# Relational graph convolution on one core: 43 of the 196 octets of layer 2 take their rows from h in the chip's memory instead of by gathers

## The chip, the cores and the metric

One NeuronCore of a Trainium2 chip runs the whole program. The metric is the device time of one execution in microseconds (us); the kernel before takes 4593.86 us (median of 3 runs, 4577.43 to 4597.59).

## The reference

There are 12,500 nodes with 128 features and 200,000 edges, sorted by destination, each with one of 8 relations. Each of two layers computes, for every node and relation, the mean of the messages that arrive there, and sums the eight means; the weights of a relation are a mix of 8 basis matrices.

```python
def _rgcn_conv(x, src, dst, et, basis, comp, root, bias):
    W = jnp.einsum('rb,bio->rio', comp, basis)
    xw = jnp.einsum('ni,rio->nro', x, W)
    msgs = xw[src, et]
    seg = dst * N_REL + et
    summed = jax.ops.segment_sum(msgs, seg, num_segments=N_NODES * N_REL)
    cnt = jax.ops.segment_sum(jnp.ones((msgs.shape[0],), x.dtype), seg, num_segments=N_NODES * N_REL)
    mean = summed / jnp.maximum(cnt, 1.0)[:, None]
    agg = mean.reshape(N_NODES, N_REL, HIDDEN).sum(axis=1)
    return agg + x @ root + bias
...
for l in range(N_LAYERS):
    h_new = _rgcn_conv(h, src, dst, edge_type, basis[l], comp[l], root[l], bias[l])
    h_new = jax.nn.relu(h_new)
    h = h_new + h
...
x = _layernorm(x + h, axis=-1)
```

## The kernel before

**Tiling.** The edges lie in 1563 columns of 128, and eight columns (1024 edges) are an octet; there are 196 octets, the last one of three columns. 98 blocks of 128 nodes cover the nodes. The edges are in the order of their destinations, so an octet reaches some 64 neighbouring nodes, and two octets about one block.

**Layer 1** (loop over o). `gather` (L651) has POOL issue eight indirect DMAs for an octet (L677), each of 128 rows of x. `onehot` (L1098) has DVE write for each column a 128x128 one-hot over (relation, one of 16 node slots), times the edge's weight 1/count (L1121), and one 128x256 one-hot `pl` (L1129) that says where the octet's node slots lie in a window of 256 nodes. `means` (L1206) multiplies rows by one-hots (PE, L1214), ACT copies the sums (`take_means`), `product` (L1238) multiplies by the eight relation matrices (L1246), `place` (L1258) adds the result into the window (L1277), and `finish` (L1285) adds bias, ReLU and residual. The new h lies in the `arena` tile as hT, features on partitions and nodes along the free axis. `table(j)` (L1335) multiplies block j of hT by all eight matrices of layer 2 in two halves of four relations (L1345, 512 columns each, through the PSUM banks pt and ct) and stores them in DRAM as `y_d`, one row for each node and relation. Halves wait in the list `tables`; from octet 50 on one is taken in each octet, and a second one while more than six wait or after octet 180. What is left over is done after the loop by `table_now`.

**Layer 2** (loop over q). An octet's eight gathers now take rows of `y_d` by 8*source + relation, so there is no product left. `slot_hots` (L1085) writes eight 128x32 one-hots (L1090) and one `pl` (L1093); `slot_sums` (L1433) adds rows into slots with eight matmuls of 32 stationary columns (L1441), four output quarters of 32 partitions, in a quarter of the bank po1 (`misc`); ACT copies them to `ys`; one octet later `place_sums` (L1451) adds them into the window (L1466), with a root matmul (L1470) in every other octet. `open_block` (L1415) copies a block of hT for that and for the residual; `norm` (L1558) turns eight finished blocks back (L1573) and normalizes them. From octet 192 on `add_rows` (L1476) does the sums.

**What sets the order.** `Plan.add` (L327) emits every instruction in program order on its engine and makes the semaphore waits from the named cells that it reads and writes. Gathers are issued five octets ahead (`gathers`, L697) into a ring of seven `rows` tiles, through four semaphore lanes `gq`, one octet each: an octet's first gather waits until the octet four before it has landed. The gathers of the last six octets of a layer also wait for PE's sums up to that point (`done`) and are issued two octets ahead. Layer 2's octets from the third on wait for all of `y_d`.

Of the kernel before, what the change touches and what calls it, by code (L numbers as in the profile page):

```python
# [300 lines left out]
class Plan:  # L301
# [90 lines left out]
    last = None  # L392
# [37 lines left out]
def ordered_path(  # L430
# [63 lines left out]
    assert FULL == NQ - 4  # L494
    main = slice(HALO, HALO + P)
# [57 lines left out]
    def h_cells(j):  # L553

        return [("h", j)] + [c for a, b, cells in over.values() if a < (j + 1) * P and b > j * P for c in cells]

    comp_sb = keep([P, L * R * NB], F32, "comp_sb")
    first = keep([P, B], F32, "first")
# [36 lines left out]

    fails = keep([P, B + 4], F32, "fails")
    fix = keep([P, 3], F32, "fix")
# [53 lines left out]
    def gather(l, q):  # L651
        if q >= NQ:
            return
# [410 lines left out]
    def check_all():  # L1064
        pt, pc = pt_b
        pb = pt.rearrange("p b t -> p (b t)")
        pe(lambda: nc.tensor.matmul(pb[0:1, :B + 4], ones, fails, start=True, stop=True),
           ["ones"] + [("fails", b) for b in range(B + 4)], [pc])
        vec(lambda: nc.vector.tensor_reduce(nb_f, pb[0:1, :B + 4], axis=AX.X, op=ALU.max), [pc], ["nb_f"])
        vec(lambda: nc.vector.tensor_copy(bad, nb_f), ["nb_f"], ["bad"])  # L1070
# [27 lines left out]
    def onehot(l, q, g=None):  # L1098

        if l == 1 and q < FULL:  # L1100
# [7 lines left out]
        if q >= NQ and (g is None or g < 0):  # L1108
            return
        emits, reads, cells = [], ["cols"], []  # L1110
# [224 lines left out]
    def table(j):  # L1335
# [29 lines left out]
        if not split:  # L1365
# [7 lines left out]
             (s_b[1][0].rearrange("p t d -> p (t d)")[:, :2 * P], s_b[1][1])]  # L1373

    sT_all = [t.rearrange("p r g k -> p (r g k)") for t in sT_r.tiles]
    yr_all = [t.rearrange("p r d -> p (r d)") for t in yr_r.tiles]
    homes = {"idx": idx.bitcast(F32), "kr": kr, "sT0": sT_all[0], "sT1": sT_all[1], "yr0": yr_all[0], "yr1": yr_all[1],
             "iota": iota_f, "dm": dm_t.rearrange("p b c -> p (b c)")}
# [7 lines left out]
    def home(where, n, *cell):  # L1386
# [4 lines left out]
        return homes[where][:, a:a + n], cell  # L1391

    dm2_t = [home("sT0", Q * 2 * K, "dm2", i) for i in range(3)]
    pl2_t = [(t, ("pl2", i)) for i, t in enumerate(pl_r.tiles)] + [home("iota", 2 * P, "pl2", 3)]
# [4 lines left out]
    dm_home_c = [c for c in old if old[c] == homes_c["dm"]]  # L1399
    dms2 = {}  # L1400
    hb_b = [(t, ("hb", i)) for i, t in enumerate((id_k, id_r, jmp.bitcast(F32)))]
    old.update({("hb", i): ["id_k", "id_r", "jmp"] for i in range(3)})
    touched = set()
# [7 lines left out]

    hb = {}
    misc = po_b[1]

    def open_block(k):  # L1415
        n = rows_of(k)
        t, c = hb_b[k % 3]
        copy(t[:, :n], hT[:, k * P:k * P + n], [("h", k)], new(c))
        plan.mark("ACT")
        hb[k] = t, c  # L1420

    def slot_numbers():
# [8 lines left out]
        plan.mark("DVE")  # L1431

    def slot_sums(q):  # L1433
        t, c = rows_g.pop((1, q))
        d, dc = dms2.pop(q)
        b, bc = misc
        m0 = b[:, 3, :]
# [13 lines left out]
    def place_sums(q, k, opens, last):  # L1451
# [4 lines left out]
        reads = [c, oc]  # L1456
        m = P
        if root_in:
# [157 lines left out]
    def sup(q):  # L1616
        return (q * Q + G) // (2 * G) - 1
# [57 lines left out]
    def checks():  # L1675
        weights(1, (pt_b, pt_b))
        yield
        for b in range(B):
            yield from check_edges(b)
        yield from check_span()  # L1680
        yield from check_place()
        yield from fix_list()

    later = checks()
# [32 lines left out]
    for o in range(NG - 3):  # L1717
# [11 lines left out]
        if parts is None:  # L1729
            run(later, 1)  # L1730
        if not opened:
# [21 lines left out]
        for i in range(2):  # L1753
            if turned_to:
                here = pt_b
                a, b = turned_to.pop(0)
            elif tables and o >= TABLE and (i == 0 or len(tables) > 6 or o > NG - 16):
                here = (pt_b, ct_b)[i]
                a, b = tables.pop(0)(here)
            else:  # L1760
                break
# [3 lines left out]
            if b is not None:  # L1765
                copies.append(b)
        plan.mark("PE")
    plan.lazy = False
# [65 lines left out]
    for q in range(2):  # L1834
        onehot(1, q)
    open_block(0)
    plan.lazy = True
# [3 lines left out]
    for q in range(NQ):  # L1841
# [38 lines left out]
        if todo:  # L1880
            todo.pop(0)()
# [90 lines left out]
```

## Time and profile before

| | |
|---|---|
| median of 3 runs | 4593.86 us |
| the profiled execution | 4590.46 us, its span 4588.4 us |
| busy in the span | PE 1941.5, DVE 1384.9, ACT 466.3, POOL 2953.3 us |
| mean granted TensorE clock | 0.665 |

The span runs from the first to the last instruction; some 2 us of the execution lie around it. PE is TensorE's matmuls, PEld its weight loads, which overlap them; DVE is VectorE, ACT is ScalarE, POOL is GpSimd, and SP issues plain DMAs. A float32 matmul shows as two records, and so does its weight load. In a row of a grouped view stand the line, engine, operation, output and inputs, shape and count, then busy time and mean length, then the idle time just before the group and what ended it. A releaser "remote", or "an unknown queue" in the chain, is here a DMA of the gathers' queue. The clock is the share of full speed that the throttle granted to TensorE.

### The profile page before, as it was taken

Reading aid. Unit: us, or ns where it says so; the run is one execution under the profiler, and the core shown is the slowest. Engines: PE = TensorE matmul, PEld = TensorE weight load, DVE = VectorE, ACT = ScalarE, POOL = GpSimd, SP = SyncE. Lnnn points to the kernel's source line nnn. Section 1 sums busy time; section 2 is a strip of 40 time slices with the busy share of each in tenths; the row PEclk is TensorE's granted clock in tenths of the full one; section 3 lists DMA queues with packets and bytes.
Section 4 is the critical chain, followed back from the end, with each engine's and each line's share of the span. In section 5 each row is a group of like instructions: output and inputs, shape, how many; then the busy total and the mean of one; then the engine's idle time right before and its main releaser. Section 6 shows DMA issues by size and latency. Waiting matters only on the chain.

```text
span 4588.4 us, 33820 instructions
## 1 busy us (share of the span) xinstructions
PE 1941.5 (42%) x11751; PEld 1512.2 (33%) x11751; DVE 1384.9 (30%) x4891; ACT 466.3 (10%) x1141; POOL 2953.3 (64%) x3135
## 2 busy tenths in 40 slices
PE   2666756666566666656731122222222222222213
PEld 1555555555455555545521111111111111111112
DVE  2544333333333323233321222222222222222224
ACT  0111112121111111111210000000000000000000
POOL 5666666666666666666556666666666666666665
PEclk9878778787777777777865555555555555555556
DMA  3111122232222222222221111212212212122121
GB/s 100 45 50 46 46 62 87 87 92 92 88 69 73 74 69 74 64 66 70 78 71 45 47 51 52 56 46 57 55 47 55 56 47 56 46 56 55 47 55 50
DMA packets 129812, 284.69 MB, mean 62 GB/s; under 512 B 54019, under 2 KB 61773, under 8 KB 129637
## 3 DMA queue, kind: packets, MB, share of 16 engines
q0 software_dynamic: 100064, 205.13, 17.2%
q10 hardware_dynamic: 16971, 52.05, 3.0%
q1 hardware_dynamic: 12602, 25.31, 1.6%
q8 instruction: 94, 1.54, 0.1%
q14 instruction: 81, 0.66, 0.0%
HBM read 223.63 MB, written 58.65 MB: 62 GB/s over the span
## 4 chain that ended last, share of the span: by engine, by line
another core or an unknown queue 64%; PE 20%; issue 8%; ACT 5%; DVE 2%; DMA 0%; POOL 0%; SPq 0%; ACTq 0%; POOLq 0%; DVEq 0%
PE y L1246 7%; PE s L1214 5%; ACT sT L627 2%; PE pt L1345 2%; PE po L1441 2%; ACT ys L627 1%; PE po L1277 1%; DVE dm L1121 1%; ACT y_row L627 1%; PE ct L1345 1%; PE ct L870 0%; PE po L1279 0%; PE ct L871 0%; PE pt L1183 0%
## 5 line engine op out<-in xcount | busy, mean ns | idle before, releaser
L677 POOL DMA_INDIRECT rows<-in_x_dram,idx x1563 | 1476.1, 944 | 841.7 <-issue 440.2
L677 POOL DMA_INDIRECT rows<-y_d,idy x1563 | 1475.1, 944 | 742.6 <-issue 453.3
L1441 PE MATMUL po<-rows,sT 128*32 128x128 f32 x3072 | 206.3, 411 | 1571.3 <-ACT ys L627 1151.2
L1246 PE MATMUL y<-w_sb,sT 128*128 128x128 f32 x3136 | 542.3, 345 | 526.2 <-ACT ys L627 198.6
L1246 PEld LDWEIGHTS y<-w_sb,sT 128*128 128x128 f32 x3136 | 509.4, 254 | 551.6 <-ACT ys L627 207.6
L1121 DVE TENSOR_SCALAR dm<-cols,kr,w 128x128 f32<-128x128 f16 x1563 | 526.2, 403 | 494.2 <-remote 203.1
L1441 PEld LDWEIGHTS po<-rows,sT 128*32 128x32 f32 x3072 | 121.9, 155 | 1658.1 <-ACT ys L627 1190.5
L1090 DVE TENSOR_SCALAR sT<-cols,kr,w 128x32 f32<-128x32 f16 x1536 | 352.8, 303 | 762.9 <-remote 617.7
L1214 PEld LDWEIGHTS s<-dm,rows 128*128 128x128 f32 x3126 | 436.3, 217 | 161.0 <-ACT sT L627 86.5
L1214 PE MATMUL s<-dm,rows 128*128 128x128 f32 x3126 | 450.5, 302 | 64.9 <-ACT sT L627 40.8
L627 ACT ACTIVATE sT<-s 128x512 f32<-128x512 f32 x391 | 212.5, 596 | 783.0 <-remote 556.8
L627 ACT ACTIVATE ys<-po 128x128 f32<-128x128 f32 x192 | 53.2, 277 | 2087.1 <-remote 1936.5
L1298 DVE TENSOR_TENSOR s<-s,carry 128x128 f32<-128x128 f32 x97 | 28.9, 298 | 670.8 <-remote 455.7
L1298 DVE TENSOR_TENSOR po<-po,carry 128x128 f32<-128x128 f32 x98 | 29.2, 298 | 655.1 <-remote 454.7
L1345 PE MATMUL pt<-w_sb,arena 128*128 128x512 f32 x258 | 157.3, 682 | 62.4 <-issue 50.0
L1466 PE MATMUL s<-pl,ys 128*128 128x256 f32 x288 | 167.9, 684 | 0.0
L1277 PE MATMUL po<-pl,ys 128*128 128x256 f32 x392 | 139.4, 440 | 24.2 <-issue 15.8
L627 ACT ACTIVATE y_row<-pt 128x512 f32<-128x512 f32 x131 | 78.4, 598 | 682.0 <-remote 484.2
L870 PE MATMUL ct<-arena,id_h 128*128 128x512 f16 (+1 forms) x188 | 75.5, 421 | 84.4 <-DVE arena L860 37.1
L860 DVE TENSOR_TENSOR arena<-cols,arena 128x129 f16<-128x129 f16 (+62 forms) x188 | 73.6, 408 | 69.5 <-remote 65.5
L1129 DVE TENSOR_SCALAR pl<-cols,pos 128x256 f32<-128x256 f16 x196 | 93.1, 476 | 0.0
L1466 PEld LDWEIGHTS s<-pl,ys 128*128 128x128 f32 x288 | 69.7, 301 | 53.3 <-issue 53.3
(212 smaller groups left out, 1409.7 us busy)
## 6 DMA issues: line engine op xcount, KB each, us to landing
y_d<-y_row ACTq DMA_DIRECT2D x96, 512.0 KB
rows<-in_x_dram,idx POOLq DMA_INDIRECT x1563
rows<-y_d,idy POOLq DMA_INDIRECT x1563
x_g<-in_x_dram SPq DMA_DIRECT2D x24, 512.0 KB
out_dram<-x_g SPq DMA_DIRECT2D x12, 512.0 KB
arena<-in_L_gnn_basis_dram SPq DMA_DIRECT2D x2, 512.0 KB
w_d<-y_row SPq DMA_DIRECT2D x2, 512.0 KB
w_sb<-w_d SPq DMA_DIRECT2D x2, 512.0 KB
```

The costliest lines, as they stand in the source:

```text
L627: act(lambda: nc.scalar.activation(out_t, in_t, AF.Copy), reads, writes)
L677: ins.append(nc.gpsimd.indirect_dma_start(out=t[:, i - q * Q, :], out_offset=None, in_=table_t, in_offset=bass.IndirectOffsetOnAxis(ap=ids ...
L870: nc.tensor.matmul(ct[:, :nb, :], id_h, eq[:, s - s0, :nb, main], start=(s == 1), stop=False)
L1090: vec(in_turn([lambda i=i: nc.vector.tensor_scalar(t[:, i, :], cols[:, :2 * K], kr[:, i0 + i:i0 + i + 1], w[:, i0 + i:i0 + i + 1], op0=ALU ...
L1121: emits.append(lambda i=i: nc.vector.tensor_scalar(t[:, i - q * Q, :wide], cols[:, :wide], ids[:, i:i + 1], w[:, i:i + 1], op0=ALU.is_equa ...
L1129: emits.append(lambda: nc.vector.tensor_scalar(o[:m], cols[:m], pos[:m, g // (2 * R), g % (2 * R):g % (2 * R) + 1], None, op0=ALU.is_equal))
L1214: last = nc.tensor.matmul(s_b[i // 4][0][:, i % 4, :], t[:, i, :], d[:, i, :], start=True, stop=True)
L1246: last = nc.tensor.matmul(y[:m], t[:, r, :nt, :].rearrange("p t k -> p (t k)"), w_sb[:, 0, r, :], start=(r == 0), stop=(r == R - 1))
L1277: ins = nc.tensor.matmul(a, o[:m], t[:m], start=opens, stop=last and not root_in)
L1345: pe(lambda: nc.tensor.matmul(hb[:n].rearrange("p r d -> p (r d)"), hT[:, j * P:j * P + n], w_sb[:, 1, k * H:(k + 1) * H, :].rearrange("p ...
L1441: last = nc.tensor.matmul(m0[i // 2 * 2 * K:(i // 2 + 1) * 2 * K, :], d[:, i, :], t[:, i, :], start=i % 2 == 0, stop=i % 2 == 1)
L1466: ins = nc.tensor.matmul(a, o[:m], t[:m], start=opens, stop=last and not root_in and not fixed)
```

## The change

In layer 2 the octets 20, 24, ..., 188 (`ROUTED`, 43 of them) issue no gathers. Their sums are formed from h itself, before the relation matrices, in these steps.

- **Sort, in layer 1** (octets 88 to 174, one half octet of four columns in each). `groups_of` compares the number of each edge's source block with 0 to 99, `earlier_of` counts with triangular and all-ones matmuls in float16 how many earlier edges of the octet have the same block, `ranks_of` takes the edge's rank and makes one-hots of 32 columns times three values (node in the block, segment, count), and `slots_of` adds these into 100 blocks x 32 slots, which two DMAs store to DRAM. Before that `values` prepares the three values. In octets 86 to 175 the second table half is not taken. `check_ranks` covers the capacity of 32 slots.
- **Turn h back** (`turn_blocks`, octets 0 to 12 of layer 2): 98 transposes put h in place as rows of nodes; `open_block` turns a block once more for its own use.
- **A unit for each routed octet**, seven steps spread over four octets from octet 13 on. A step has four tiles of four blocks (the seventh has one tile of two blocks). `compare` makes one-hots of 32 columns for 16 blocks at once (128x512) from a broadcast of the slots' node numbers (`fetch`, 128 times 6400 bytes); `pick_rows` has 16 matmuls with 32 stationary columns that pick each slot's row of h; `slots_in` makes for each tile a 128x640 one-hot over two batches of 512 edges, 8 relations and 40 node slots, times the weight; `add_up` multiplies each tile by the two halves of it (320 columns) into two PSUM banks; after the 25th tile ACT copies both, and `relate` multiplies by the eight relation matrices. `place_sums` then takes 80 instead of 128 slots.
- `slot_sums` writes to the bank ct instead of po1.

```diff
+    BT = 4
+    CAP = 32
+    NW = 40
+    BU = P // CAP
+    NTL = -(-NT // BU)
+    TU = 4
+    NU = -(-NTL // TU)
+    NGR = NTL * BU
+    SEG = R * NW
+    BR = 2
+    EVERY = 4
+    TURN = 8
+    FROM = -(-NT // TURN)
+    ROUTED = list(range(FROM + 10 * EVERY // NU + 2, 192, EVERY))
+    NR = len(ROUTED)
+    SORT = 88
...
     def gather(l, q):
-        if q >= NQ:
+        if q >= NQ or l == 1 and q in ROUTED:
             return
...
+    def groups_of(x):
...
+        vec(lambda: nc.vector.tensor_tensor(
+            o3, cols[:, None, :NGR].to_broadcast([P, BT, NGR]), g.unsqueeze(2).to_broadcast([P, BT, NGR]),
+            op=ALU.is_equal), ["cols", grp_b[1]], [oc])
...
+    def earlier_of(x):
...
+        def emit():
+            last = nc.tensor.matmul(c3, tri, o3, start=True, stop=False)
+            for k in range(BT if h else 0):
+                nc.tensor.matmul(c3, every, f3[:, k:k + 1, :].to_broadcast([P, BT, NGR]), start=False, stop=False)
+            for k in range(1, BT):
+                last = nc.tensor.matmul(c3[:, k:, :], every, o3[:, :BT - k, :], start=False, stop=k == BT - 1)
+            return last
...
+    def ranks_of(x):
...
+        vec(lambda: nc.vector.tensor_tensor(c3, b3, o3, op=ALU.mult), [bc, oc], [cc])
+        vec(lambda: nc.vector.tensor_reduce(rk, c3, axis=AX.X, op=ALU.add), [cc], [rc])
+        vec(lambda: nc.vector.tensor_tensor(
+            j3, cols[:, None, :CAP].to_broadcast([P, BT, CAP]), rk.unsqueeze(2).to_broadcast([P, BT, CAP]),
+            op=ALU.is_equal), ["cols", rc], [jc])
+        vec(lambda: nc.vector.tensor_tensor(
+            v4, j3[:, :, None, :].to_broadcast([P, BT, 3, CAP]),
+            val[:, j, ts].unsqueeze(3).to_broadcast([P, BT, 3, CAP]), op=ALU.mult), [jc, val_b[1]], [vc])
...
+    def compare(t):
+        i, u = t // NU, t % NU
...
+        vec(lambda: nc.vector.tensor_scalar(o[:, :n], b.bitcast(F16)[:, u * HC:u * HC + n], node_p, None,
+                                            op0=ALU.is_equal), [bc, "node"], new(oc))
+
+    def slots_in(t):
...
+        for v, m in tiles_at(u):
+            o, oc = slot_b[(i * NTL + v) % len(slot_b)]
+            n = m * CAP
+            vec(lambda v=v, o=o, n=n: nc.vector.tensor_scalar(
+                o[:n], segs[:n], sg[:n, v:v + 1], sg[:n, NTL + v:NTL + v + 1], op0=ALU.is_equal, op1=ALU.mult),
+                [segs_b[1], sgc], new(oc))
+
+    def pick_rows(t):
...
+        b, bc = pt_b
+        def emit():
+            for x, (v, m) in enumerate(at_u):
+                for k in range(m):
+                    j = v * BU + k
+                    n = rows_of(j)
+                    c = (x * BU + k) * CAP
+                    last = nc.tensor.matmul(b[k * CAP:(k + 1) * CAP, x, :], o[:n, c:c + CAP],
+                                            hT[:n, j * P:(j + 1) * P], start=True, stop=True)
+            return last
...
+        copy(g[:m, :n * P], b[:m, :n, :].rearrange("p t d -> p (t d)"), [bc], new(gc))
+
+    seg_b = [y_full, po_b[0]]
+
+    def add_up(t):
...
+            for x, (v, m) in enumerate(at_u):
+                o, n = slot_b[(i * NTL + v) % len(slot_b)][0], m * CAP
+                for k, (b, _) in enumerate(seg_b):
+                    last = nc.tensor.matmul(b.rearrange("p t d -> p (t d)")[:, :SEG], g[:n, x * P:(x + 1) * P],
+                                            o[:n, k * SEG:(k + 1) * SEG], start=v == 0, stop=v == NTL - 1)
...
+    def route_step(t):
+        i, u = t // NU, t % NU
+        if u == 0 and i < NR:
+            unit_rows(i)
+        compare(t + 1)
+        if i < NR:
+            pick_rows(t)
+        if 0 <= t - 1 < NR * NU:
+            slots_in(t - 1)
+        if 0 <= t - 2 < NR * NU:
+            add_up(t - 2)
+        if u == 3 and i >= 1 and i - 1 < NR:
+            relate(i - 1)
+        if u == 1:
+            fetch_rows(i + 1)
+        if u == NU - 1:
+            fetch(i + 2)
+
+    steps_of = {}
+    for t in range(NR * NU + 5):
+        steps_of.setdefault(FROM + t * EVERY // NU, []).append(t)
...
     def slot_sums(q):
...
-        b, bc = misc
+        b, bc = ct_b
...
             elif tables and o >= TABLE and (i == 0 or len(tables) > 6 or o > NG - 16):
+                if i == 1 and SORT - 2 <= o < SORT + 2 * NR + 2:
+                    break
...
+        if 0 <= o - SORT < 2 * NR:
+            earlier_of(o - SORT)
+        if 0 <= o - SORT - 1 < 2 * NR and (o - SORT) % 2 == 0:
+            slots_of((o - SORT) // 2 - 1)
...
+        turn_blocks(q)
+        if q == FROM - 1:
+            compare(0)
+        route(q, 0)
         late = q - 1
-        if q < FULL:
+        if q < FULL and q not in ROUTED:
             slot_sums(q)
         if 0 <= late < FULL:
             place_sums(late, sup(late), *opened_by(late))
         if q >= FULL:
             add_rows(q, k, opens, last)
+        route(q, 1)
         onehot(1, q + 2)
         if sup(q + 2) != sup(q + 1) and q + 2 < NQ:
             open_block(sup(q + 2))
+        route(q, 2)
```

More of the change, by code (lines that the diff above doesn't have):

```diff
@@ L1108, in onehot @@
         if q >= NQ and (g is None or g < 0):
+            return
+        if l == 1 and q in ROUTED:
+            i = ROUTED.index(q)
+            o, c = pl[q] = pl2_r.take()
+            vec(lambda: nc.vector.tensor_scalar(o[:2 * NW], cols[:2 * NW], pos2[:2 * NW, i:i + 1], None,
+                                                op0=ALU.is_equal), ["cols", "pos2"], new(c))
+            plan.mark("DVE")
             return
@@ L1391, in home, with spare @@
         return homes[where][:, a:a + n], cell
+    def spare(n, *cell):
+        old[cell] = room_c + [rank_b[1] + (x,) for x in range(2 * NR)]
+        return later_on(n), cell
+    bits_b = [spare(NGR * CAP // 2, "bits", i) for i in range(2)]
+    hot_b = [home("dm", HC, "hot", i) for i in range(3)]
+    rows_b = [home("dm", HC, "picked", i) for i in range(3)]
+    slot_b = [spare(2 * SEG, "slot", i) for i in range(5)]
+    slot_b += [home(("sT1", "idx", "idx")[i], 2 * SEG, "slot", 5 + i) for i in range(3)]
+    sum_b = [home(("yr0", "yr1")[i], R * BR * NW, "sum", i) for i in range(2)]
+    segs_b = home("yr1", SEG, "segs")
+    rows2_b = [home("dm", P, "rows2", i) for i in range(2)]
     dm2_t = [home("sT0", Q * 2 * K, "dm2", i) for i in range(3)]
@@ new lines, in ordered_path, with relate @@
+    for i in range(2):
+        for k in range(BR):
+            old[sum_b[i][1] + (k,)] = old[sum_b[i][1]]
+    def relate(i):
+        t_s, sc = sum_b[i % 2]
+        t4 = t_s.rearrange("p (r b n) -> p r b n", r=R, b=BR)
+        b, bc = misc
+        pe(in_turn([lambda r=r: nc.tensor.matmul(
+            b[:BR * NW, 0, :], t4[:, r].rearrange("p b n -> p (b n)"), w_sb[:, 1, r, :], start=r == 0, stop=r == R - 1)
+            for r in range(R)]), [sc + (k,) for k in range(BR)] + [("w", 1, r) for r in range(R)], [bc])
+        plan.mark("PE")
+        o, c = ys[ROUTED[i]] = ys_r.take()
+        copy(o[:BR * NW], b[:BR * NW, 0, :], [bc], [c])
+        plan.mark("ACT")
```

273 lines of the change are left out of this document (263 added, 10 removed).

## The prediction

> **What bounds the kernel now.** I read the page first, then layer 2 by stretches.
>
> ```profile
> span 4588.4 us, 33820 instructions
> ...
> PEclk9878778787777777777865555555555555555556
> ...
> L677 POOL DMA_INDIRECT rows<-y_d,idy x1563 | 1475.1, 944 | 742.6 <-issue 453.3
> ```
>
> The profiled execution took 4590.46 us, 2.1 us more than this span and 3.4 us less than the median of the runs shown. My sum is made against it. From about the middle the granted clock is 0.5, and POOL has one kind of work, the gathers. The next rows are two stretches of the view by stretches (busy us of PE, PEld, DVE, ACT, POOL, then clock, DMA share, GB/s): the steady part of layer 2, and ten microseconds at the end of layer 1.
>
> ```profile
> 2600.00:4400.00 1800.00, 399.47 (x3104) 246.06 (x3103) 466.55 (x1936) 62.93 (x249) 1196.61 (x1269) 0.52 0.19 52
> 2240.00:2250.00 10.00, 10.00 (x71) 8.37 (x70) 6.12 (x20) 4.68 (x10) 0.00 (x0) 1.00 0.18 72
> ```
>
> In layer 2 PE is busy 22% of the time at a clock of 0.52, DVE 26%, ACT 3%. In 1800 us there are 1269 gathers, one in 1.418 us, so an octet of eight takes 11.35 us. The groups of that stretch say why:
>
> ```profile
> L677 POOL DMA_INDIRECT rows<-y_d,idy x1269 | 1197.6, 944 | 603.7 <-issue 367.3 <-remote 234.9 <-PE po L1441 0.6
> ```
>
> A gather costs 0.944 us plus 0.29 us of issue (367.3/1269), some 9.9 us an octet. The other 1.5 us an octet (234.9 over 158.6 octets) is the wait for the octet four before to land. Everything else waits for these gathers. The stretch that the change replaces runs from octet 13's sums to octet 187's:
>
> ```profile
> L1441 PE MATMUL po<-rows,sT 128*32 128x128 f32 x2784 | 187.7, 413 | 1385.5 <-ACT ys L627 1051.4 <-issue 299.5 <-DVE x_g L1581 34.6
> ```
>
> ```profile
> 2559.20 0.46 PE L1441 MATMUL po<-rows,sT 128*32 128x128 f32 x4
> ```
>
> ```profile
> 4512.84 0.67 PE L1441 MATMUL po<-rows,sT 128*32 128x128 f32 x16
> 4513.43 0.70 PE L1466 MATMUL s<-pl,ys 128*128 128x256 f32 x2
> 4513.97 0.38 PE L1470 MATMUL s<-jmp,w_sb 128*128 128x128 f32 x2
> 4514.28 0.66 PE L1441 MATMUL po<-rows,sT 128*32 128x128 f32 x16
> ```
>
> The first row is the group of `slot_sums` in that stretch, the others are its ends in the order of time (start and length in us). At 16 records an octet these are 174 octets, in 4514.3 - 2559.2 = 1955.1 us: 11.24 us each.
>
> **The change: what goes.** 43 of these octets lose eight gathers. Were gathers all, 131 octets at 11.35 us would take 1487 us and 468 us would go. Four octets would need 34.0 instead of 45 us. But PE has to do a whole unit in the same four octets, so PE's work must be priced, and at the clock that it then has.
>
> **The price of a matmul.** At 2240 us PE is dense, and its clock is 1.00. The order of time there:
>
> ```profile
> 2240.14 1.02 PE L1345 MATMUL ct<-w_sb,arena 128*128 128x512 f32 x2
> 2241.00 1.95 PE L1214 MATMUL s<-dm,rows 128*128 128x128 f32 x16
> 2242.78 1.95 PE L1246 MATMUL y<-w_sb,sT 128*128 128x128 f32 x16
> 2244.57 0.60 PE L1277 MATMUL po<-pl,ys 128*128 128x256 f32 x2
> 2245.00 1.02 PE L1345 MATMUL pt<-w_sb,arena 128*128 128x512 f32 x2
> ```
>
> Start to start (a length also holds the drain), a float32 matmul (two records) over 512 columns takes 0.86 us, over 256 0.43, over 128 0.223 (1.78 for eight). It goes with the columns, so 320 columns take 0.5375 us. Weight loads hide. For 32 stationary columns I take octet 186, in the four rows from 4512.84 us above; the view by stretches has it at full clock too:
>
> ```profile
> 4512.84:4514.88 2.04, 2.04 (x38) 1.47 (x37) 2.04 (x10) 0.28 (x1) 0.00 (x0) 1.00 0.00 0
> ```
>
> Sixteen such records take 0.59 us, where one after the other they would need 16 x 0.111 = 1.78 us. So the four output quarters run side by side, 0.028 us a record. The matmuls after them take 0.54 and 0.31 us instead of 0.43 and 0.22; this switch between narrow and full belongs to the block, which costs 0.79 us.
>
> **PE's sum.** Per unit: `pick_rows` has six blocks of 32 records, 0.79 + 16 x 0.028 = 1.24 us each, and a small one of 0.6, together 8.0 us. `add_up` has 25 tiles x 2 = 50 matmuls over 320 columns, 26.9 us. `relate` has eight of 128, 1.8, and `unit_rows` about 0.2. That makes 36.9 us, and 43 units 1587 us. Beside them, in the same 174 octets: 131 `slot_sums` at 0.79, 103 us; 174 `place_sums` at 0.43, 75; a root matmul and the new turn of `open_block` in every other octet, 87 x 0.44, 38; the transposes of `norm`, eight in 16 octets, 19. All of it is **1822 us** at full clock, 41.9 us in four octets, against 1955 now. Against 34 us of gathers PE sets the pace, and gathers run ahead of it.
>
> **What PE waits for on top.** Matmuls of a step follow an order laid out by hand. `pick_rows(t)` needs the one-hot that DVE made a step before, `add_up(t-2)` a copy by ACT two steps old and one-hots that DVE could begin two steps before, as eight slot tiles hold two steps. A step is six microseconds of PE, so these have time; what is queued behind PE's waits, the next gather octet's sums, has landed by then. The places where PE must wait are the shared banks: `misc` after an `open_block` or a `norm` turn (the reader's 0.3 to 0.7 us, a few times a unit) and pt after the short seventh step, whose picks wait for ACT's copies of two banks and one of 0.6 us. No row has such waits; bounds are nothing and one step's one-hots from DVE, 2.2 us, plus those, some 3.5 us. I take **1.5 us a unit**, 65 us, since each wait is short and the queue orders agree.
>
> **DVE and ACT beside it.**
>
> ```profile
> L1121 DVE TENSOR_SCALAR dm<-cols,kr,w 128x128 f32<-128x128 f16 x1563 | 526.2, 403 | 494.2 <-remote 203.1 <-PE pt L1345 94.8 <-PE ct L1345 79.4
> L1090 DVE TENSOR_SCALAR sT<-cols,kr,w 128x32 f32<-128x32 f16 x1536 | 352.8, 303 | 762.9 <-remote 617.7 <-PE po L1441 64.5 <-PE s L1466 53.6
> ...
> L1581 DVE TENSOR_TENSOR x_g<-po,x_g 128x512 f32<-128x512 f32 x24 | 16.6, 692 | 159.6 <-PE po L1573 98.5 <-remote 53.6 <-issue 7.5
> ...
> L832 DVE CAST arena<-arena 128x512 f32<-128x512 int32 x3 | 1.2, 415 | 0.0
> ...
> L1427 DVE TENSOR_SCALAR idx<-idx 128x1664 int32<-128x1664 int32 x1 | 1.0, 1028 | 0.0
> ```
>
> ```profile
> L1601 DVE TENSOR_SCALAR x_g<-x_g,st 128x128 f32<-128x128 f32 x8 | 2.1, 363 | 0.0
> ```
>
> Between SBUF tiles a column costs 0.53 ns ((1028-415)/1152), and eight two-scalar operations of 128 columns take 2.1 us. So 640 columns in `slots_in` take 0.27 + 512 x 0.53 = 0.54 us. No row has float16 in and float32 out between SBUF tiles; from PSUM (L1090, L1121) a column costs 1.04 ns, which makes 0.87 us the upper bound. I take 0.54, as the operands lie in SBUF. A unit then costs DVE 25 x 0.54 = 13.6, seven comparisons at 0.42 = 2.9, and the octets' own work, 2.94 us each in the stretch of 1800 us, less a routed octet's eight one-hots (8 x 0.23): 9.9 us. Together 26 us of 42, or 36 by the upper bound. ACT gets seven copies of 0.6 us and some short ones, 7 us of 42. Both are hidden while their order holds.
>
> **Layer 1.**
>
> ```profile
> 1000.00:1800.00 800.00, 494.78 (x2637) 412.05 (x2636) 254.02 (x808) 139.88 (x301) 526.22 (x558) 0.77 0.26 77
> ...
> 2320.00:2340.00 20.00, 1.67 (x7) 0.76 (x5) 0.00 (x0) 0.28 (x1) 14.88 (x17) 0.61 0.20 53
> ```
>
> 558 gathers in 800 us make 11.5 us an octet; PE is busy 7.1 and DVE 3.6 us of it. The sort adds five DVE operations of 128 to 400 columns, some 2.6 us by L1581's 692 ns, and on PE a mean of 1800 float16 columns and half of eight short matmuls, some 1.5 us. DVE reaches 6.2 and PE 8.6 of 11.5, so the gathers hide both. The list of table halves, counted octet by octet from the two rules, stands at 26 instead of 7 in octet 172, and at 12 instead of none after the loop. Ten halves more at 0.86 us of PE and 0.6 us of ACT are some 15 us; PE is idle for 18 of 20 us at 2320, where it waits for the last gathers, so most of it is hidden. I add **8 us** for that and the small preparations (bounds 0 and 20). The broadcast of 0.8 MB a unit is small beside a DMA share of 0.19.
>
> **The sum.** 4588.4 - 1955.1 + 1822 + 64.5 + 8 = 4527.8, and 2.1 around the span: **4530 us**, 1.3% below 4590.5.
>
> **Two rules of the skill.** The Trainium skill's page "TensorE: Matmul & The Clock Gate" (What's actually happening) says that TensorE starts throttled to half speed and is released by some 3.4 us of activity; the rows at 0.52 and 1.00 agree, and by that rule a dense unit keeps 1.00. "SBUF — State Buffer" (Who interferes with whom), also in the Trainium skill, speaks against the change: a VectorE operation between SBUF tiles in a two-port mode locks GpSimd out entirely while it runs.
>
> **Rivals.**
>
> *The clock falls back* (12%). PE's waits in each step are spread, and the dense stretch shown at 1.00 is ten microseconds long. In layer 1, with PE busy 62%, the clock is 0.77. The streaming part goes with 1/clock: at 0.9 it takes 2025 us, and the time is 4733; at 0.77, 2367, and 5075. It decides below 0.97. Against it: PE's work is 96% of the new stretch.
>
> *PE and DVE in lockstep* (18%). DVE works strictly in order, and operations of `finish` and `norm` that wait for PE stand ahead of `slots_in`. If in each unit PE waits out one whole step's one-hots and the banks, 3.7 us, the time is 4530 + 43 x 2.2 = 4625, slower; with the upper bound for DVE (four at 0.87, so 5 us) 4681. It decides from 2.9 us a unit, 0.4 us a step. For it: one order, three engines. Against it: DVE has 16 us to spare.
>
> *The gathers are held up by DVE* (5%). If POOL stands still in every operation between SBUF tiles, a unit's 24 gathers at 1.24 us and 16.5 us of such operations make 46.3 us, 11.6 for each octet of the stretch: 174 octets take 2014 us, the time is 4657. That is the page's rule on the two ports at its full. The trace shows little of it:
>
> ```profile
> 2930.20 2.14 DVE L1601 TENSOR_SCALAR x_g<-x_g,st 128x128 f32<-128x128 f32 x8
> 2930.88 0.99 POOL L677 DMA_INDIRECT rows<-y_d,idy  x1 [0.30 <-issue]
> 2932.18 0.98 POOL L677 DMA_INDIRECT rows<-y_d,idy  x1 [0.31 <-issue]
> ```
>
> Under eight such operations in a row, two gathers took 0.99 and 0.98 instead of 0.94 us.
>
> *It doesn't do what it says* (2%). If a check of the sort (32 slots a block, 40 nodes a batch) fails, the program runs the general path behind it; at four indirect DMAs a column, 6252 at 1.24 us, that adds over 7700 us. Some 10 edges a block make this unlikely.
>
> **How the numbers follow.** The forecast, PE dense at full clock with 0 to 3.5 us of waits a unit, has 62% (4457 to 4616), and 1% is left for what I don't see. A measurement of this kernel can tell about 0.5% from no change, 23 us: the forecast's part below 4567 needs waits under 2.4 us a unit, 50%; the rest of it, 12%, is within; the rivals, all above, 38% slower. The range goes from the sum with no waits and nothing for layer 1 (4457) to 4710, which holds the lockstep whole and leaves out the clock below some 0.91 and the general path.
>
> **What would show it.** Right: between octets 13 and 187 PE is busy over 90% at a clock near 1.00, L1441 takes about 0.6 us a block, `add_up` 0.54 us a matmul, POOL waits for PE, and the stretch is some 1890 us long. The first half ends within 10 us of 2320. Wrong: PE idle over 3 us a unit behind DVE, a granted clock under 0.97, gathers longer than 1.2 us, or `pick_rows` at 0.1 us a record, which would mean that its quarters don't run side by side.

## The result, and the profile after

The changed kernel takes 4876.39 us, the kernel before 4590.73 us in the same runs (medians of four each): a ratio of 1.0623, with a 95% interval from 1.0587 to 1.0659. It is 6.2% slower, and the time lies above the whole range of the prediction. The profiled execution took 4872.19 us. The page of the changed kernel:

```profile
span 4870.1 us, 63642 instructions
...
PEclk6888777877778777778757999999999999999997
...
L728 POOL DMA_INDIRECT rows<-y_d,idy x1219 | 1187.1, 974 | 1318.4 <-PE ct L1860 925.9
```

The mechanism is the one that was forecast: 344 gathers are gone, and in layer 2 POOL now waits for PE (L1860 is `slot_sums`) and no longer the other way round. The next row is the view by stretches for 1600 us of the steady part (busy us of PE, PEld, DVE, ACT, POOL, then clock, DMA share, GB/s):

```profile
2700.00:4300.00 1600.00, 1448.74 (x11923) 978.07 (x11922) 841.83 (x2395) 198.76 (x483) 743.05 (x758) 0.94 0.19 54
```

PE is idle for 151 of 1600 us, and its clock is 0.94. The ends of the replaced stretch, octets 13 and 187, in the order of time:

```profile
2593.35 0.37 PE L1860 MATMUL ct<-rows,sT 128*32 128x128 f32 x1 [2.43 <-issue]
...
4789.64 0.66 PE L1860 MATMUL ct<-rows,sT 128*32 128x128 f32 x16
```

The stretch is 2196.3 us long, where 1886.5 were forecast and the kernel before had 1955.1. (The expectations below say 2193; they end it at octet 186.) Octet 13 begins 34.2 us later than before (2559.20), and what follows the start of octet 187's sums takes 80.5 us in place of 74.1. These three, 241.2 + 34.2 + 6.3, are the 281.7 us between the spans. So the question is why PE, whose work was priced at 1822 us, needs 374 us more.

PE's own rows say where it is idle. Of the 151 us, 115.9 lie before or inside the blocks of picks (`pick_rows`, L1753):

```profile
L1753 PE MATMUL pt<-arena,dm 128*32 128x128 f32 x6142 | 261.9, 285 | 115.9 <-issue 65.2 <-ACT dm L678 48.6
```

"ACT dm" is ACT's copy of the picks before, which must have emptied the bank pt. Of the 65.2 us put down to "issue", some 48 lie inside a block, in 84 pauses of up to 1 us, where no matmul waits for another engine. So there are two kinds of idle time, and the first is followed here.

The order of time shows one wait for that copy:

```profile
3420.15 1.08 PE L1753 MATMUL pt<-arena,dm 128*32 128x128 f32 x32
...
3422.43 0.33 PE L1678 MATMUL po<-ident,arena 128*128 128x128 f32 x1
...
3424.11 0.60 ACT L678 ACTIVATE dm<-pt 128x512 f32<-128x512 f32 x1 [4.14 <-PE po L1678]
...
3424.76 1.08 PE L1753 MATMUL pt<-arena,dm 128*32 128x128 f32 x32 [2.00 <-ACT dm L678]
```

The block of picks (L1753) is over at 3421.23. ACT has nothing to do, yet its copy of the picked rows begins at 3424.11, 2.9 us later, and the next picks, which need the same bank, stand still for 2.00 us. ACT's group of these copies in the stretch above:

```profile
L678 ACT ACTIVATE dm<-pt 128x512 f32<-128x512 f32 (+1 forms) x221 | 121.8, 551 | 714.5 <-remote 406.2 <-PE pt L1753 137.0 <-PE po L1678 129.3
```

Most of the wait is put down to "remote": a signal came, and no instruction of the core had just ended. The trace's semaphore events say the same. Between 2600 and 4700 us 1051 matmuls post a signal, and the trace has 1020 events of it; matched in order, with the least lag that fits, 419 come over 1 us after the matmul's end, and the mean is 1.3 us. Those of ACT and DVE come after 0.01 us in the mean. A "late signal" is here this time between the end of a matmul's record and its event. The ends are modelled, so a matmul that really ends later than its record would look the same.

Not every signal is late. ACT begins the copies of picks 2.1 us in the mean after both the picks' end and its own last instruction, but its copies of `slot_sums` within 0.1 us, all 95 of them:

```profile
L678 ACT ACTIVATE ys<-ct 128x128 f32<-128x128 f32 x95 | 26.3, 277 | 330.2 <-PE ct L1860 330.2
```

So it isn't ACT that is slow to wake.

The kernel before has late signals too, in rows that the prediction didn't read:

```profile
3030.47 1.10 PE L1441 MATMUL po<-rows,sT 128*32 128x128 f32 x16 [11.46 <-issue]
...
3044.28 0.28 ACT L627 ACTIVATE ys<-po 128x128 f32<-128x128 f32 x1 [13.67 <-remote]
...
3044.51 0.94 POOL L677 DMA_INDIRECT rows<-y_d,idy  x1 [4.37 <-remote]
...
3044.61 1.10 PE L1441 MATMUL po<-rows,sT 128*32 128x128 f32 x16 [11.46 <-ACT ys L627]
```

```profile
L627 ACT ACTIVATE ys<-po 128x128 f32<-128x128 f32 x159 | 44.0, 277 | 1734.8 <-remote 1599.0 <-PE po L1441 66.9 <-issue 60.8
```

The sums of an octet end at 3031.57; ACT's copy of them begins 12.7 us later, and POOL stands for 4.37 us, since the octet's rows may not be overwritten before. POOL's other condition, the landing of the octet four before, was met long ago: the last event of that lane is at 3005.89. So "remote" in POOL's row is not a DMA of the gathers' queue, as the legend ahead of the prediction has it, but PE's late signal. The second fence is ACT's group from 2600 to 4400 us: nearly all of its wait is "remote". Its 159 copies begin 9.3 us in the mean after the sums' end.

### The profile page after: what moved, and what is told of

Same layout as the page of the kernel before. It is cut to its first block, busy times and chain, and to the rows that moved or that the text cites. A ratio compares the mean times of both kernels' runs of the same rounds, so it can differ in the third digit from the quotient of the medians.

```text
span 4870.1 us, 63642 instructions
## 1 busy us (share of the span) xinstructions
PE 3594.7 (74%) x25583; PEld 2636.0 (54%) x25583; DVE 2246.8 (46%) x6511; ACT 701.1 (14%) x1640; POOL 2673.8 (55%) x2791
## 4 chain that ended last, share of the span: by engine, by line
PE 62%; another core or an unknown queue 22%; issue 9%; ACT 4%; DVE 2%; DMA 0%; POOL 0%; ACTq 0%; POOLq 0%; DVEq 0%
PE y L1774 14%; PE po L1774 13%; PE y L1304 8%; PE pt L1753 7%; PE s L1272 5%; PE s L1885 2%; ACT sT L678 2%; PE pt L1403 2%; PE ct L1860 2%; PE po L1796 2%; PE po L1335 1%; PE po L1678 1%; ACT y_row L678 1%; PE ct L1527 1%
## 5 line engine op out<-in xcount | busy, mean ns | idle before, releaser
L728 POOL DMA_INDIRECT rows<-y_d,idy x1219 | 1187.1, 974 | 1318.4 <-PE ct L1860 925.9
L1774 PE MATMUL y<-arena,dm 128*128 128x320 f32 (+1 forms) x1346 | 532.1, 478 | 8.2 <-issue 7.6
L1774 PE MATMUL po<-arena,dm 128*128 128x320 f32 (+1 forms) x1346 | 502.3, 456 | 0.7 <-issue 0.6
L1753 PE MATMUL pt<-arena,dm 128*32 128x128 f32 x8428 | 362.1, 285 | 165.6 <-issue 98.4
L1753 PEld LDWEIGHTS pt<-arena,dm 128*32 128x32 f32 x8428 | 238.0, 112 | 261.6 <-issue 149.6
L1723 DVE TENSOR_SCALAR arena<-y_row,comp_sb 128x640 f32<-128x640 f16 (+1 forms) x347 | 202.5, 626 | 333.0 <-PE po L1774 249.8
L1774 PEld LDWEIGHTS po<-arena,dm 128*128 128x128 f32 (+1 forms) x1346 | 273.3, 203 | 122.7 <-issue 26.0
L1774 PEld LDWEIGHTS y<-arena,dm 128*128 128x128 f32 (+1 forms) x1346 | 258.8, 204 | 146.3 <-issue 68.2
L1774 PE MATMUL y<-idx,dm 128*128 128x320 f32 (+1 forms) x536 | 211.3, 476 | 3.5 <-issue 2.6
L1774 PE MATMUL po<-idx,dm 128*128 128x320 f32 (+1 forms) x536 | 200.2, 457 | 0.0
```

The source lines that it names most:

```text
L728: ins.append(nc.gpsimd.indirect_dma_start(out=t[:, i - q * Q, :], out_offset=None, in_=table_t, in_offset=bass.IndirectOffsetOnAxis(ap=ids ...
L1723: vec(lambda v=v, o=o, n=n: nc.vector.tensor_scalar(o[:n], segs[:n], sg[:n, v:v + 1], sg[:n, NTL + v:NTL + v + 1], op0=ALU.is_equal, op1=A ...
L1753: last = nc.tensor.matmul(b[k * CAP:(k + 1) * CAP, x, :], o[:n, c:c + CAP], hT[:n, j * P:(j + 1) * P], start=True, stop=True)
L1774: last = nc.tensor.matmul(b.rearrange("p t d -> p (t d)")[:, :SEG], g[:n, x * P:(x + 1) * P], o[:n, k * SEG:(k + 1) * SEG], start=v == 0, ...
```

## The theories, and the chips

**Theory A** is that of late signals: while gathers are under way, PE's signals reach the other engines microseconds late; PE then waits for the copies that hang on them, and its pauses cost it the full clock. **Theory B**: the clock drops by itself under these matmuls. **Theory C**: PE and DVE work in lockstep, as in the second rival.

Kernels that were timed together ran on one chip, and the experiments fell on four chips. On two of them the kernel before takes about 4587 us, as in the result above; on the other two it takes 3927. Each experiment says which. The runs on the second kind decide more than any edit.

## Experiments on the signals

**Most gathers left out** (a chip on which the kernel before takes 4587 us).

```
         i0, n = q * Q, in_quad(q)
+        if l == 1 and 20 <= q < 187:
+            n = 1
```

> The changed kernel with seven of eight gathers of each octet from 20 to 186 of layer 2 left out (the sums then run over rows left in the buffers; all other work is kept). Theory A, late signals: while gathers are under way, the signals by which PE tells ACT, DVE and POOL that a block is done arrive 2 to 5 us late, the next picks wait for the copy behind them, and the pauses cost clock. Then PE's pauses go to under 1 us a unit, the clock of the stretch is 0.98 or more, and 174 octets take 1830 to 1900 us in place of 2193: about 4550 to 4600 us. Theory B, the clock drops by itself under these matmuls: it stays near 0.94 and the time above 4750. Theory C, PE and DVE in lockstep: PE still pauses about 5 us a unit behind DVE, 4800 to 4870.

It took 4502.93 us. The stretch is 1840.7 us, and in 1600 us of it (view by stretches, then ACT's group):

```profile
2700.00:4300.00 1600.00, 1589.63 (x14318) 1106.27 (x14310) 998.71 (x2875) 236.64 (x581) 116.84 (x114) 1.00 0.10 32
```

```profile
L678 ACT ACTIVATE dm<-pt 128x512 f32<-128x512 f32 (+1 forms) x266 | 146.4, 550 | 462.3 <-PE pt L1755 460.9
```

PE is busy 99% at a clock of 1.00, and ACT's wait now ends with the picks. B and C fall: the same matmuls and the same DVE work run without pauses. PE's sum of 1822 us is right to 1%.

**POOL busy without gathers.** In place of the seven gathers left out, POOL fills 896 columns with zeros seven times an octet, and PE's sums wait for the fills.

```
+            if busy:
+                for _ in range(7):
+                    pool(lambda: nc.gpsimd.memset(t[:, 1:, :], 0.0), [], [cell + (2,)])
```

> As few_gathers, which took 4503 us with PE busy 99% and no late signals, but in place of each gather left out POOL fills 896 columns of the octet's rows with zeros, so that POOL is busy about as long without issuing a gather. If PE's signals come late because POOL is busy, the lags of 2 to 5 us and the time of the changed kernel come back, 4750 to 4900. If they come late because of what a gather sets off (its descriptors and transfers), PE stays dense and the time is 4490 to 4560.

This run fell on a chip on which the kernel before takes 3927 us: 4016.28 us, with prompt signals. As the changed kernel itself has prompt signals there (below), it tells nothing. The second run:

> The kernel of pool_busy again (POOL fills zeros in place of seven of eight gathers), in the hope of a chip on which the kernel before takes about 4587 us. There: 4490 to 4560 us with prompt signals if it is the gathers that hold PE's signals up, 4750 to 4900 with late ones if it is POOL being busy. On a chip where before takes 3927 us, 4010 to 4020 again, which tells nothing new.

This one fell on a chip where the kernel before takes 4587.58 us, and took 4500.94 us (stretch 1839.9 us):

```profile
2700.00:4300.00 1600.00, 1589.64 (x14323) 1106.34 (x14321) 1284.29 (x2873) 236.87 (x581) 892.38 (x912) 1.00 0.10 32
```

```profile
L752 POOL MEMSET rows<- 128x896 f32 x798 | 771.6, 967 | 39.4
```

POOL is busier than in the changed kernel (892 against 743 us), each fill takes 967 ns, as long as a gather, and PE is dense. What holds the signals up on such a chip is the gathers, not POOL being busy. Whether it is their descriptors or their transfers was not separated.

**Both kernels on a chip of the second kind.**

> The kernel before, unchanged, for its trace: its runs beside the second set of kernels took 3927 us, beside the first 4587. If the late signals of PE are what differs between the two chips, a run near 3930 shows PE's signals within 0.1 us of the last matmul, octets of 9.96 us (eight gathers at 1.245) and no wait of POOL for PE; a run near 4590 shows them late again, 1 us or more in half of the cases. Theories B and C say nothing of a difference between chips.

> The changed kernel, unchanged. Theory A: on a chip where the kernel before takes 3927 us, PE is dense at full clock, 174 octets in 1822 to 1850 us in place of 1733 for gathers at 9.96, with 7 to 35 us of transition and tail: 4020 to 4070 us, a ratio of 1.024 to 1.036, still slower. On a chip where it takes 4587 us, 4860 to 4890 as before. Theory B, the clock by itself, or C, lockstep: PE pauses 5 us a unit and runs at 0.94 on either chip, 4330 to 4400 where before takes 3927.

The kernel before took 3927.67 us (profiled), the changed one 4016.01 us, a ratio of 1.0224 (1.0207 to 1.0241). The kernel before, 1200 us of layer 2, with POOL's and ACT's groups there:

```profile
2200.00:3400.00 1200.00, 308.29 (x2336) 193.83 (x2336) 352.83 (x1459) 48.06 (x189) 907.15 (x962) 0.50 0.23 60
```

```profile
L677 POOL DMA_INDIRECT rows<-y_d,idy x962 | 907.7, 944 | 293.2 <-issue 293.2
```

```profile
L627 ACT ACTIVATE ys<-po 128x128 f32<-128x128 f32 x120 | 33.2, 277 | 1151.1 <-PE po L1441 1086.0 <-issue 65.1
```

A gather takes 944 ns, as on the first chip, and 305 ns of issue, and nothing else: 962 in 1200 us, an octet in 9.98 us in place of 11.35. "Remote" is gone from POOL and ACT. The changed kernel, the same view and groups, then the ends of its stretch:

```profile
2200.00:3400.00 1200.00, 1189.17 (x10700) 827.30 (x10698) 775.36 (x2165) 177.20 (x434) 696.38 (x722) 1.00 0.23 67
```

```profile
L1753 PE MATMUL pt<-arena,dm 128*32 128x128 f32 x5501 | 195.8, 276 | 0.0
```

```profile
2128.75 0.86 PE L1860 MATMUL ct<-rows,sT 128*32 128x128 f32 x10 [5.41 <-DMA rows<-y_d,idy]
...
3948.79 0.66 PE L1860 MATMUL ct<-rows,sT 128*32 128x128 f32 x16
```

With all its gathers PE is busy 99% at 1.00, picks never wait, and the stretch is 1820.0 us. None of PE's 1028 signals on record between 2200 and 3900 us is over 0.3 us late. In the kernel before the same octets take 1737.5 us there:

```profile
2105.25 0.89 PE L1441 MATMUL po<-rows,sT 128*32 128x128 f32 x12 [7.33 <-DMA rows<-y_d,idy]
...
3842.75 0.89 PE L1441 MATMUL po<-rows,sT 128*32 128x128 f32 x12 [7.25 <-DMA rows<-y_d,idy]
```

So the 241.2 us that the stretch lost in the result split in two. With prompt signals the change costs 1820.0 - 1737.5 = 82.5 us, because four octets of gathers need 4 x 9.98 = 39.9 us and PE's work in them 41.9. The first kind of chip costs the kernel before 1955.1 - 1737.5 = 217.6 us there, and the changed kernel 2196.3 - 1820.0 = 376.3: 158.7 more. That all of this comes by late signals is not shown; the pauses inside picks are part of the 376.3.

Layer 1 has it too. Of the 662.9 us between the two spans of the kernel before, 454.0 lie ahead of octet 13 (2559.20 against 2105.25). There ACT's copies of the sums of `means` wait for "remote" on the first kind, and on the second not at all (the kernel before, the view of waits: us, times, longest):

```profile
ACT sT L627 <- remote: 556.8, 93, 13.8
```

## Experiments on the change's parts

**Units left out**, the sort kept (second kind of chip; `relate` and the fetches stay).

```
         i, u = t // NU, t % NU
-        if u == 0 and i < NR:
-            unit_rows(i)
...
-            add_up(t - 2)
```

> The changed kernel with the sort kept, but the units left out of layer 2 (no picks, no one-hots of columns, no sums of a unit; the 43 octets still get no gathers, and their place_sums run on old data). What is left of the stretch is 131 octets of gathers. At the 11.35 us an octet of the kernel before: 1487 us, 706 less than in the changed kernel, 4166 us in all. If the 34 us by which octet 13 began later come from the sort and the table halves, it still begins at about 2590; if they come from the first units, near 2560, and 4130 in all. A pace of 10 us an octet (1310) would mean that gathers themselves can go faster than the kernel before showed.

3522.27 us. The stretch is 1318.4 us for 131 octets, 10.06 each: the gathers' own pace, once more without the 1.4 us. Octet 13 begins at 2127.0 us, as in the changed kernel (2128.75) and 22 us later than before: on this kind that delay belongs to the sort and the table halves, not to the units. Where it arises is seen in POOL's groups from 2300 to 2420 us of the first chip, before and after:

```profile
L677 POOL DMA_INDIRECT rows<-y_d,idy x52 | 49.1, 944 | 16.1 <-issue 16.1
...
L673 POOL DMA_INDIRECT jmp<-y_d,fix_i x1 | 0.9, 939 | 34.0 <-DMA y_d<-y_row 34.0
```

```profile
L728 POOL DMA_INDIRECT rows<-y_d,idy x36 | 34.0, 944 | 42.8 <-DMA y_d<-y_row 32.2 <-issue 10.7
...
L724 POOL DMA_INDIRECT jmp<-y_d,fix_i x1 | 0.9, 938 | 16.2 <-DMA y_d<-y_row 16.2
```

The table halves left over hold up the first gather of layer 2 by 32.2 us, where before it waited for nothing but its issue. Part of that comes back, as the gather of the fixed rows then waits 16.2 us in place of 34.0. Octet 13's first gather is issued 21.6 us later (2518.00 against 2496.37); the rest of the 34.2 us arises between that gather and PE's sums, on the first kind alone.

**Two banks for picks** (first kind of chip; the first edit is in `slot_sums`, the second in `pick_rows`).

```
-        b, bc = ct_b
+        b, bc = misc
...
-        b, bc = pt_b
+        b, bc = (pt_b, ct_b)[t % 2]
```

> The changed kernel with the picks of odd steps in the bank of slot_sums, and slot_sums back in the bank that it had before. Theory A, late signals: a copy that begins 2 to 5 us late no longer holds up the next picks, which come 6 us later; of the 213 us of pauses in the stretch the 150 us ahead of picks mostly go, and with them some of the 130 us of half clock: 4600 to 4720 us. New waits in the bank that slot_sums now shares could give back up to 2 us a unit. Theory B, the clock by itself: pauses go, clock does not, 4720 to 4800. Theory C, lockstep with DVE: no change, 4850 to 4900.

4827.64 us, 1.0521 of the kernel before (1.0486 to 1.0555): 49 us better than the changed kernel, not 156 to 276. The picks no longer wait for ACT, and the clock rises from 0.94 to 0.97, but PE still stands in them:

```profile
2700.00:4300.00 1600.00, 1459.27 (x12078) 977.90 (x12076) 856.10 (x2429) 202.08 (x490) 761.33 (x772) 0.97 0.19 55
```

```profile
L1753 PE MATMUL ct<-arena,dm 128*32 128x128 f32 x3104 | 136.5, 279 | 32.3 <-issue 32.3
L1753 PE MATMUL pt<-arena,dm 128*32 128x128 f32 x3104 | 134.9, 277 | 39.8 <-issue 39.5
```

These 72 us are idle time inside the blocks of picks, for which the profile shows no wait ("issue"), as some 48 us in the changed kernel; on the second kind, and without gathers, that idle time is nought. So late copies are not all that such a chip takes from PE. What these pauses are was not found.

**POOL waits for ACT's copy** (first kind of chip).

```
-        copy(o, m0, [bc], [oc])
+        copy(o, m0, [bc, c + (0,), c + (1,)], [oc])
```

> The changed kernel in which POOL waits for the copy of an octet's sums by ACT before it refills the octet's rows, so that it waits on ACT's semaphore and no longer on PE's. If PE's signals come late because POOL waits on the same semaphore, the copies of picks begin within 0.5 us and the time falls to 4560 to 4650. If they come late beside gathers whoever waits (theory A), the lags stay and the time is within 0.5% of the changed kernel, 4850 to 4900; theories B and C say the same.

4729.66 us in its one run, 147 us below the changed kernel, which neither side expected. Signals over 1 us late fall from 316 of 778 to 211 of 736 (2600 to 4200 us), and those that are late remain 2 to 6 us late: that POOL waits on the same semaphore isn't the cause. The gathers now begin 0.3 us later against PE's order, and with that other signals meet them. That is argued, not shown, and below, with fewer units, this edit and the one before together gain nothing.

## A unit less often

The runs say that PE is the bound and the gathers have room, so a unit may come less often.

```
-    EVERY = 4
+    EVERY = 6
```

> The changed kernel with a unit in each six octets in place of four (29 units). PE then needs 36.9 + 5 x 0.79 + 6 x 0.43 + 3 x 0.44 + 0.7 = 45.4 us at full clock in six octets, gathers 5 x 11.35 = 56.7 us. Theory A: PE with 5 to 8 us of waits and half clock still stays below the gathers, which set the pace again: 29 x 56.7 + 34 of transition, about 4310 us, up to 4400 if the gathers wait behind units for PE's late signals. Theory B: a clock near 0.8, as in layer 1, makes PE's part 57 us, as long as the gathers, 4310 to 4420. Theory C: a fixed 15 us a unit more makes 60 us in six octets, 4410.

> A unit in each six octets, no other edit. Where the kernel before takes 3927 us: gathers 49.8 us in six octets, PE 45.4, so 1444 to 1480 for the stretch, and the same 3640 to 3680 us as with the two edits for late signals, since there they have nothing to hide. Where it takes 4587 us: 4450 to 4480 again.

> A unit in each six octets, with the two banks for picks and with POOL waiting for ACT's copy of an octet's sums. Alone these gave -119 us against the kernel before, -45 and -147 against the changed kernel. If the late signals are what is left (every6 took 62.7 us in six octets, where gathers need 56.7 and PE 45.4), the two edits bring it towards 57 to 60 us: 4300 to 4390 us. If the pace of every6 is set by the gathers' own issue, they change nothing: 4440 to 4490.

> The same with the two banks for picks and POOL waiting for ACT. Where the kernel before takes 3927 us: 3655 to 3670 again. Where it takes 4587 us: 4300 to 4440, 30 to 150 us below every6 alone if the two edits hide late signals.

> A unit in each six octets with both edits against late signals. On a chip where before takes about 4587 us: 4300 to 4440 if the edits hide late signals, 4440 to 4480 if not. On one where it takes 3927 us: 3655 to 3670 again.

> The same with a unit in each five octets (34 units): gathers need 45.4 us, PE 43.8 at full clock. With 5 us of waits and half clock for a tenth of the time PE takes some 51 to 53 us in five octets, 1790 to 1840 for the stretch, 4430 to 4490 us. If late signals cost as much a unit as in the changed kernel (8.5 us), 4470 to 4530.

| unit in each | other edits | chip where before takes | time (us) | ratio (95%) |
|---|---|---|---|---|
| 6 octets | none | 4586.57 | 4467.89 | 0.9735 (0.9701 to 0.9768) |
| 6 octets | both | 4587.58 | 4482.34 | 0.9763 (0.9747 to 0.9779) |
| 6 octets | none | 3926.82 | 3663.02 | 0.9325 (0.9309 to 0.9341) |
| 6 octets | both | 3927.47, 3926.82 | 3660.83, 3661.52 | 0.9323 (0.9307 to 0.9338) |
| 5 octets | both | 3927.47 | 3696.10 | 0.9413 (0.9397 to 0.9429) |

A unit in each six octets is faster than both kernels on either kind of chip. With prompt signals it is what the sum says: the gathers set the pace, with no wait but their issue (POOL's group, then the view by stretches with a unit in each six octets and no other edit; last the same view with a unit in each five, where PE is the bound again):

```profile
L728 POOL DMA_INDIRECT rows<-y_d,idy x948 | 911.2, 961 | 288.9 <-issue 284.0 <-PE pt L1753 1.8 <-PE po L1774 1.5
```

```profile
2200.00:3400.00 1200.00, 1095.21 (x9904) 760.10 (x9908) 791.68 (x2370) 168.97 (x437) 911.16 (x948) 0.96 0.28 78
```

```profile
2200.00:3400.00 1200.00, 1178.27 (x10793) 820.29 (x10786) 828.75 (x2384) 183.62 (x459) 883.36 (x912) 1.00 0.27 77
```

Where signals are late, the gain is less than half of that, and 4310 to 4400 us was expected. The stretch takes 1836.8 us in place of 1644, 63.3 us in six octets. Neither engine is full; POOL waits 324 of 1600 us for PE's sums or its late signals:

```profile
L728 POOL DMA_INDIRECT rows<-y_d,idy x1017 | 984.8, 968 | 617.4 <-issue 273.5 <-PE ct L1860 201.6 <-remote 122.6
```

There both edits together change nothing for the better (4482 against 4468, on two chips of that kind): picks stand 113 us as "issue" in 1600 us, and in the bank that `slot_sums` now shares, its sums and the transposes of `open_block` wait 38.8 and 37.4 us for ACT. Theory A was wrong in that a second bank would hide what the signals cost.

## Why the prediction was wrong, point by point

- **What bounds the kernel now**: here it failed first. "The other 1.5 us an octet (234.9 over 158.6 octets) is the wait for the octet four before to land": it isn't. It is POOL's wait for PE's late signals, and on a chip where they are prompt an octet takes 9.98 us. The row of L1441 with "1385.5 <-ACT ys L627 1051.4" was quoted, and it says that PE waits 1051 us for a copy of 0.28 us, and the step didn't ask what the copy waits for. The prediction had both numbers of the rival that it didn't write: gathers without that wait at "some 9.9 us an octet", so less than 40 us for four, and 41.9 us of PE. If the wait goes, the change is slower by these two alone.
- **The price of a matmul, and PE's sum**: right. 1820.0 us were measured where nothing holds PE up, 1840.7 with few gathers; 1822 were forecast. Picks run side by side in four quarters, 32 records in 1.08 us.
- **What PE waits for on top**: the term that failed in the result. 1.5 us a unit, 65 us, were taken, with 3.5 as the upper bound. In 1600 us PE was idle for 151, so some 208 us in the stretch, 4.8 us a unit; its busy time, some 1989 us, is 167 above the sum, and the clock of 0.94 explains some 120 of that. Together they are the 374. The step said that "no row has such waits". Rows had: the "remote" of ACT's copies in the kernel before. On the second kind of chip the whole term is nought.
- **The clock falls back**, a rival at 12%: it fell, to 0.94, but as a consequence of the pauses and not by itself; without them it is 1.00, as the Trainium skill's page "TensorE: Matmul & The Clock Gate" (What's actually happening) says of a dense PE.
- **PE and DVE in lockstep** (18%) had nearly the right idle time, 3.7 to 5 us a unit, by the wrong cause: PE waits for ACT, and ACT for PE's signal, or PE pauses with no wait shown. That is luck. **The gathers are held up by DVE** (5%): a gather takes 0.974 us after in place of 0.944; the full lock of that rule is not seen.
- **Layer 1**: 8 us were taken, with an upper bound of 20. It was 34.2 us on the first chip and 23.5 with prompt signals. The idle PE at 2320 us was taken for cover, but the first gather of layer 2 waits for the tables, and it had no slack.
- **The sum**: the range (4457 to 4710) covered wrong prices of what was seen, not a bound that was misread. A slower kernel had 38%, but by rivals that the runs don't show.

A page of the Trainium skill bears on the reading: "Perfetto Trace Analysis" (Summary: the profiler window per engine type) says that the profile's end of a TensorE instruction is an estimate, and that the passing of its semaphore isn't in it. The traces agree: a record of the picks is 285 ns long on the first kind of chip and 276 on the second, and only the events and the waits of others show the 1.3 us.

**What stays open**: why two of four chips deliver PE's signals late beside gathers and two don't; why in the changed kernel those of picks are late and those of `slot_sums` not; and what the pauses without a wait inside the picks are. On the first kind the trace also lacks events: of the 956 signals of PE in the kernel before it has 843 there and 946 on the second kind. Whether the recording itself has a part in the lateness is not shown.

## What to carry to other kernels

Before a bound is priced, follow each long wait to its end: an engine that waits 1000 us for a copy of 0.28 us, and a release put down to "remote", are questions to settle and not costs to take over. When work moves from one engine to another, compare what the two would need if neither waited (here 39.9 against 41.9 us), and choose how much to move so that both stay under the bound; a third less of the change gained 2.6 to 6.8% where all of it lost. And time both kernels on more than one chip when a wait has no visible cause.

## What the runs showed of the hardware

- One program, the kernel before, takes 4587 us on two chips and 3927 us on two others, 17% apart, with gathers of the same length (944 ns, and on the second kind 305 ns of issue and nothing else).
- On the first kind, beside gathers, PE's signals come 1.3 us after the modelled end in the mean in layer 2 of the changed kernel; in the kernel before ACT's copies begin 9.3 us after the sums' end in the mean, 12.7 us in the case shown, and 0.1 us on the second kind. Signals of ACT and DVE come after 0.01 us in the mean. With seven of eight gathers left out, or replaced by fills of 967 ns, PE's come after 0.03 us in the mean on the same kind of chip.
- On that kind alone, PE also stands inside dense blocks of small matmuls, some 48 of 1600 us in the changed kernel and 72 with two banks, with no wait that the profile shows.
